# Down projection with a zero-padded last weight chunk kept twice, and int8 staging replaced by int16 in place

## The chip, the cores and the metric

The kernel runs on one core of a Trainium2 chip. The metric is the device time of one execution in microseconds; the profile is one further execution, recorded by the hardware profiler. TensorE (PE) multiplies, VectorE (DVE), ScalarE (ACT) and GpSimd (POOL) work on elements, SyncE (SP) issues DMAs. A line number such as L1046 is a line of the kernel's file as profiled before.

## The reference, cut to what matters

The input x is 64 sequences of 64 tokens with 256 channels. A rotation, a decayed linear attention with its residual and a pooled softmax over tokens come first; then a feed-forward layer, quantized to 8-bit integers, is added to x. This last part is what the change touches:

```python
xq = _act_fake_quant(x, clip_x[0])
gate = jnp.einsum('bsh,ih->bsi', xq, _weight_fake_quant(w_gate))
up = jnp.einsum('bsh,ih->bsi', xq, _weight_fake_quant(w_up))
h = _act_fake_quant(jax.nn.silu(gate) * up, clip_down[0])
return jnp.einsum('bsi,hi->bsh', h, _weight_fake_quant(w_down))
```

`_act_fake_quant` takes one scale over the whole tensor (sigmoid of the clip factor, times the largest magnitude, over 127), divides, rounds, clips to -128 to 127 and multiplies by the scale again. `w_gate` and `w_up` are 704 x 256, `w_down` is 256 x 704. The integers are exact in bf16, so the matmuls run on bf16 integers and the scales are applied afterwards.

## The kernel before

The 4096 tokens are cut into 8 groups (`NG`) of 512 tokens (`GW`), each 4 tiles of 128 tokens. The attention phase works through the groups in a hand-written order, with the preparation of the weights spread over its steps: `weight_round` (ACT, to int8), `weight_widen` (DVE, int8 to bf16) and `weight_transpose` (PE, with ACT copying the result out of PSUM). `w_down` is the third of them and comes last, in the step near 131 us.

The inner width of 704 is cut into 6 chunks (`NC`): five of 128 rows and a last one of 64 (`LAST`). Groups are paired: pair j holds groups 2j and 2j + 1. The inner layer of a pair lies in `hT[j]`, 11 rows (`NF + 1`) of 128 partitions x 512 tokens in f32: rows 0, 2, 4, 6, 8 are the five full chunks of the even group, rows 1, 3, 5, 7, 9 those of the odd group, and row 10 (`NF`) holds the 64-row last chunk of the even group on partitions 0 to 63 and that of the odd group on partitions 64 to 127. The quantized copy `hq[j]` has the same layout in bf16; its pool keeps two such tiles, so pair j + 2 takes the place of pair j. The down weights `wdT` lie in chunks of 128 partitions x 256 outputs; their last chunk holds the 64 rows twice, on both halves of the partitions.

Before the down projection the feed-forward part multiplies gate and up. Its input integers come from `quantize_tokens`: ACT multiplies by the inverse scale and writes int8 (L959), and DVE (groups 0 and 1) or POOL (the others) widens to bf16 (L961). The largest magnitude of the inner layer is collected on DVE; `act_scale` turns it into `sh` and its inverse `rh`. Only then can the down projection begin:

- `quantize(g)`: ACT multiplies `hT` by `rh` and writes int8 into `h8` (L1046); DVE widens that into `hq` (L1047). The even group also does row 10 for both groups, as a separate instruction of its own. The first group is cut into 1, 1 and 2 token tiles, the last into 2 and 2; all others are done at once.
- `down(g)`: for each of 4 token tiles, 6 matmuls (L1060) accumulate over the chunks, the last with only 64 rows of the array. Two tiles share a PSUM tile `pdn` (4 buffers). DVE multiplies each by the output scale `dsc` (L1067) into the residual's tile. For groups 0 to 6 POOL issues an accumulating DMA onto the output (L1076), which the attention phase has already stored; for group 7 DVE adds the residual (L1072) and SP issues two plain stores (L1073).

The order on ACT, DVE and POOL is that of the code (`manual_schedule`): `quantize(g)` is written ahead of `down(g - 1)`, so on DVE the widening of group g stands ahead of the two evictions of group g - 1. PE's order and all waits come from the framework, which follows what each instruction reads and writes.

Of the kernel before, what the change touches and what calls it, by code (L numbers as in the profile page):

```python
# [10 lines left out]
BF16 = mybir.dt.bfloat16  # L11
I32 = mybir.dt.int32
I8 = mybir.dt.int8
AF = mybir.ActivationFunctionType
ALU = mybir.AluOpType
AX = mybir.AxisListType

P = 128
NEG = -1e30
QMAX = 127.0  # L20
# [6 lines left out]
def adaln_attn_ffn(  # L27
# [20 lines left out]
    nc = tc.nc  # L48
    B, S, D = x.shape
# [3 lines left out]
    FF = w_gate.shape[0]  # L53
# [4 lines left out]
    GW = GT * P  # L58
# [3 lines left out]
    NC = (FF + P - 1) // P  # L62
    LAST = FF - (NC - 1) * P
# [4 lines left out]
    const = ctx.enter_context(tc.tile_pool(name="const", bufs=1))  # L68
# [20 lines left out]

    wgT = const.tile([P, 2, FF], BF16, name="wgT")  # L90
    wuT = const.tile([P, 2, FF], BF16, name="wuT")
    wdT = const.tile([P, NC, D], BF16, name="wdT")
    wscale = const.tile([P, 2, NC], F32, name="wscale")
    dsc = const.tile([P, D], F32, name="dsc")

# [14 lines left out]
    with ExitStack() as actx:  # L110
# [22 lines left out]
        pooled = [pool_a[:, g] if g < 5 else pool_b[:, g - 5] for g in range(NG)]  # L133
# [8 lines left out]
        def scale_ys(g):  # L142
            if g == 0:

                ys = pool.tile([P, GT, D], F32, tag="ys", name="ys_0", bufs=1)
                for t in range(GT):
                    nc.scalar.activation(
                        ys[:, t], xg[0][:, t], AF.Copy, scale=cs[:, 1, t : t + 1]
                    )
# [67 lines left out]
        def keys(g):  # L217
# [3 lines left out]
            for r in range(2):  # L221
                pk = by_token(g, r, wkT, "pk")
                sq = pool.tile([P, 512], F32, tag="sq", name=f"sq_{g}_{r}")
                nc.scalar.activation(sq, pk, AF.Square)
                nc.vector.tensor_reduce(
# [312 lines left out]
        with tc.tile_pool(name="prep", bufs=1) as prep:  # L538
# [22 lines left out]
            for k in range(2):  # L561
                rows = slice(k * A, (k + 1) * A)
# [9 lines left out]
            row, tok = p32("row", 1), p32("tok", 1)  # L572
# [3 lines left out]
            for k in range(P // 32):  # L576
                rows = slice(32 * k, 32 * (k + 1))
                V.tensor_scalar_add(row[rows], sq32[rows, 0:1], 32.0 * k)
            V.tensor_scalar(ident, col, row, None, ALU.is_equal)
            for k in range(2):  # L580
                rows = slice(k * S, (k + 1) * S)
# [32 lines left out]
            for k in range(2):  # L614
                rows = slice(k * S, (k + 1) * S)
# [48 lines left out]
            w, pt = turn(wkT, wq_nat, center, 2)  # L664
# [3 lines left out]
            w, pt = turn(wqT, wq_nat, ident, 0)  # L668
# [24 lines left out]
            for k in range(2):  # L693
                rows = slice(k * S, (k + 1) * S)
# [5 lines left out]
            w, pt = turn(wvT, wq_nat, ident, 4)  # L700
# [14 lines left out]
            w, pt = turn(woT, wo_nat, ident, 0)  # L715
# [6 lines left out]
            for k in range(2):  # L722
                half = slice(k * A, (k + 1) * A)
                V.tensor_scalar_mul(vb[half, half], ones[half, half], v1s[half])

        wprep = actx.enter_context(tc.tile_pool(name="wprep", bufs=1))


        full = (NC - 1) * P
        wnat, wint = [], []  # L730
        for j, w in enumerate((w_gate, w_up)):
# [17 lines left out]
        w8 = [  # L749
            wprep.tile(list(nat.shape), I8, tag="w8", name=f"w8_{j}")  # L750
            for j, nat in enumerate(wnat)
# [19 lines left out]
        def weight_widen(j):  # L771
            if j < 2:
                q = wprep.tile([P, NC, D], BF16, tag="wq", name=f"wq_{j}")
                nc.vector.tensor_copy(q, w8[j])
            else:
                q = wprep.tile([P, 2, NC * P], BF16, tag="wq", name="wq_d")
                nc.vector.tensor_copy(q[:, :, 0:FF], w8[j])
                nc.vector.tensor_copy(q[:, :, FF : NC * P], q[:, :, full:FF])

                for hc in range(2):  # L780
                    nc.vector.tensor_scalar_mul(
                        wnat[2][:, hc, 0:P], ident, sd[:, hc : hc + 1]
                    )
                nc.vector.memset(wnat[2][:, 0, P : 2 * P], 1.0)
            wint.append(q)

        def weight_transpose(j):
            q = wint[j]
            if j < 2:
                for kc in range(2):  # L790
                    pt = ps.tile([P, 1024], BF16, tag="bank", name=f"pw_{j}_{kc}")
                    for c in range(NC):
                        n = P if c < NC - 1 else LAST
                        nc.tensor.transpose(
                            pt[:, c * P : c * P + n],
                            q[:n, c, kc * P : (kc + 1) * P],
                            identb[:n, :n],
                        )
                    nc.scalar.copy((wgT, wuT)[j][:, kc, :], pt[:, :FF])
                return  # L800
            pd = bank("pdsc")
            for hc in range(2):
                nc.tensor.matmul(
                    pd[:, hc * P : (hc + 1) * P],
                    wnat[2][:, 0, P : 2 * P],
                    wnat[2][:, hc, 0:P],
                    start=True,
                    stop=True,
                )
            nc.scalar.copy(dsc, pd[:, :D])  # L810
            for hc in range(2):
                pt = ps.tile([P, 1024], BF16, tag="bank", name=f"pwd_{hc}")
                for c in range(NC):
                    nc.tensor.transpose(
                        pt[:, c * P : (c + 1) * P], q[:, hc, c * P : (c + 1) * P], identb
                    )
                nc.scalar.copy(
                    wdT[:, :, hc * P : (hc + 1) * P],
                    pt[:, : NC * P].rearrange("p (c h) -> p c h", h=P),
                )  # L820


        for step in range(1, NG):
            p, a, q = step, step - 1, step - 2
# [52 lines left out]
        a, q = NG - 1, NG - 2  # L877
# [42 lines left out]
        rx = const.tile([P, 1], F32, name="rx")  # L920
# [3 lines left out]
    with ExitStack() as fctx:  # L924
# [5 lines left out]
        NF = 2 * (NC - 1)  # L930
        ps_f = ctx.enter_context(ExitStack())
        fw = ps_f.enter_context(tc.tile_pool(name="ffnw", bufs=2))
# [3 lines left out]
        xq = fp.tile([P, 2, NT], BF16, name="xq")  # L936
        hT = [
            (fp if j < NP - 1 else big).tile(
                [P, NF + 1, GW], F32, tag=f"hT{j}" if j < NP - 1 else "last", name=f"hT{j}"
            )  # L940
            for j in range(NP)
        ]
# [10 lines left out]
        )  # L953
        wsx = fp.tile([P, 2, NC], F32, name="wsx")

        def quantize_tokens(g, kcs=slice(0, 2)):

            x8 = fw.tile([P, 2, GW], I8, tag="x8", name=f"x8_{g}_{kcs.start}", bufs=4)
            nc.scalar.activation(x8[:, kcs], pooled[g][:, kcs], AF.Copy, scale=rx)  # L959
            widen = nc.vector if g < 2 else nc.gpsimd  # L960
            widen.tensor_copy(xq[:, kcs, g * GW : (g + 1) * GW], x8[:, kcs])  # L961

        for kc in range(2):
            for g in range(2):
# [14 lines left out]
        for j in range(NP):  # L979
            for c in range(NC):  # L980
# [4 lines left out]
                for dst, w in ((pg, wgT), (pu, wuT)):  # L985
                    for kc in range(2):
                        for k in range(2):
                            g = 2 * j + k
# [11 lines left out]
                h = hT[j][:, 2 * c : 2 * c + n, :]  # L1000
# [18 lines left out]
        fw = fctx.enter_context(tc.tile_pool(name="ffnd", bufs=2))  # L1019
# [5 lines left out]
        rh = fp.tile([P, 1], F32, name="rh")  # L1025
# [3 lines left out]
        hq = {}  # L1029

        def quantize(g):

            j, k = divmod(g, 2)
            if k == 0:
                hq[j] = fw.tile([P, NF + 1, GW], BF16, tag="hq", name=f"hq_{j}")

            h8 = fw.tile([P, NC, GW + 64], I8, tag="h8", name=f"h8_{g}")
            at = 0
            for n in (1, 1, 2) if g == 0 else (2, 2) if g == NG - 1 else (4,):
                cols = slice(at * P, (at + n) * P)  # L1040
                at += n
                for rows, tmp in (
                    (slice(NF, NF + 1), h8[:, NC - 1 : NC, cols]),
                    (slice(k, NF, 2), h8[:, 0 : NC - 1, cols]),
                )[k:]:
                    nc.scalar.activation(tmp, hT[j][:, rows, cols], AF.Copy, scale=rh)  # L1046
                    nc.vector.tensor_copy(hq[j][:, rows, cols], tmp)  # L1047

        def down(g):
            j, k = divmod(g, 2)  # L1050

            res = xg[0 if g == NG - 1 else g]
            for r in range(2):
                tiles = slice(2 * r, 2 * r + 2)
                pdn = ps_d.tile([P, 2, D], F32, tag="pdn", name=f"pdn_{g}_{r}")
                for i in range(2):
                    tok = slice((2 * r + i) * P, (2 * r + i + 1) * P)
                    for c in range(NC):
                        half = slice(0, P) if c < NC - 1 else slice(k * LAST, (k + 1) * LAST)
                        nc.tensor.matmul(  # L1060
                            pdn[:, i, :],
                            hq[j][half, 2 * c + k if c < NC - 1 else NF, tok],
                            wdT[half, c, :],
                            start=(c == 0),
                            stop=(c == NC - 1),
                        )
                nc.vector.tensor_tensor(  # L1067
                    res[:, tiles], pdn, dsc.unsqueeze(1).to_broadcast([P, 2, D]), ALU.mult
                )
                if g == NG - 1:  # L1070
                    xr = xg[g][:, tiles, :]
                    nc.vector.tensor_tensor(xr, xr, res[:, tiles], ALU.add)  # L1072
                    nc.sync.dma_start(out=ot[g][:, tiles, :], in_=xr)  # L1073
            if g < NG - 1:

                nc.gpsimd.dma_start(out=ot[g], in_=res, accum_op=ALU.add)  # L1076
# [53 lines left out]
```

## Time and profile before

| | us |
|---|---|
| median of 3 runs | 336.67 (335.77 to 337.44) |
| profiled execution, its own time | 336.96 |
| its span in the profile | 335.2 |
| down projection: from the first ACT instruction of `quantize` to the last DVE add | 296.83 to 330.50 |
| last output data landed | 334.0 |

Busy time over the whole span: PE 286.9 us (86%), DVE 244.2 (73%), ACT 197.6 (59%), POOL 84.9 (25%). The span is what lies between the first and the last instruction on the core; the execution's own time is 1.8 us longer. The shares are means over stages that differ: the down projection is the last tenth of the span, so it has to be read by itself. Matmuls overlap, so their mean duration is longer than their distance; the distance is read from their starts.

### The profile page before, as it was taken

The numbers are of one execution on the slowest core, as the hardware profiler recorded it, in microseconds if no ns is written. First come the engines' busy times: TensorE is split into PE (matmuls) and PEld (weight loads), VectorE is DVE, ScalarE is ACT, GpSimd is POOL, SyncE is SP. The second block draws the span as 40 slices with busy tenths as digits, with TensorE's granted clock in tenths as the row PEclk, the third lists the DMA queues.
The fourth block names the chain that finished last, engine by engine and source line by source line (L and its number), as shares of the span: only waits on it lengthen the run. The fifth ranks groups of instructions, "written<-read, shape, count | busy, mean of one in ns | idle before, by whom it ended". The sixth has DMA issues, their size and how long they took to land.

```text
span 335.2 us, 8697 instructions
## 1 busy us (share of the span) xinstructions
PE 286.9 (86%) x3760; PEld 194.9 (58%) x3764; DVE 244.2 (73%) x510; ACT 197.6 (59%) x303; POOL 84.9 (25%) x76
## 2 busy tenths in 40 slices
PE   0599999999999999989999999975498898549992
PEld 0386768668658758848858858653333243115551
DVE  5669886886976985794894694765528789968883
ACT  1566458567476573774574574323668988559820
POOL 0051330240230221014003003040037746503541
PEclk9999999999999999999999999998589999958997
DMA  5590711001001000100100200200000000001999
GB/s 156 128 350 19 218 60 62 5 2 65 3 2 61 8 0 5 62 3 3 65 2 2 66 2 0 68 1 3 0 2 0 1 0 2 0 0 17 164 154 166
DMA packets 16789, 16.15 MB, mean 48 GB/s; under 512 B 2160, under 2 KB 16496, under 8 KB 16752
## 3 DMA queue, kind: packets, MB, share of 16 engines
q1 hardware_dynamic: 12480, 11.83, 11.4%
q0 software_dynamic: 3696, 3.67, 8.2%
q8 instruction: 29, 0.48, 0.6%
q10 hardware_dynamic: 576, 0.11, 0.2%
q14 instruction: 8, 0.07, 0.1%
HBM read 7.74 MB, written 7.86 MB: 47 GB/s over the span
## 4 chain that ended last, share of the span: by engine, by line
PE 53%; DVE 21%; ACT 15%; issue 5%; DMA 3%; POOL 2%; ACTq 0%; DVEq 0%
PE po L388 9%; PE pv L208 9%; PE pdn L1060 7%; PE pk L208 6%; PE psc L323 4%; PE py L361 4%; DVE at L336 4%; ACT gate L997 3%; ACT L238 3%; PE pl L511 3%; DMA afb<-n_L_cond_amplitudes_dram 3%; PE pa L433 2%; POOL hT L1006 2%; ACT up L1003 2%; DVE xam L528 2%
## 5 line engine op out<-in xcount | busy, mean ns | idle before, releaser
L336 DVE TENSOR_TENSOR at<-psc,gam 128x512 f32<-128x512 f32 x64 | 39.6, 680 | 14.6 <-PE psc L323 14.6
L154 POOL TENSOR_TENSOR ys<-x,cs 128x1024 f32<-128x1024 f32 x7 | 13.8, 1967 | 89.3 <-DVE xr L168 67.6
L388 PE MATMUL po<-woT,yT 128*128 128x256 f32 x128 | 31.1, 386 | 5.2 <-DVE kn L254 2.7
L1006 POOL TENSOR_TENSOR hT<-gate,up 128x1024 f32<-128x1024 f32 x10 | 23.7, 2370 | 37.3 <-ACT up L1003 37.3
L1060 PE MATMUL pdn<-wdT,hq 128*128 128x256 bf16 x192 | 30.1, 291 | 3.0 <-DVE hq L1047 3.0
L208 PE MATMUL pk<-wkT,xT 128*128 128x256 f32 x128 | 30.2, 390 | 0.2 <-ACT xT L198 0.2
L989 PE MATMUL pg<-xq,wgT 128*128 128x512 bf16 (+1 forms) x94 | 25.9, 399 | 4.7 <-DVE xq L961 2.2
L208 PE MATMUL pv<-wvT,xT 128*128 128x256 f32 x128 | 29.8, 386 | 0.1
L388 PEld LDWEIGHTS po<-woT,yT 128*128 128x128 f32 x128 | 23.1, 190 | 11.2 <-DVE kn L254 5.1
L283 PE MATMUL pq<-xT,wqT 128*128 128x512 f32 x64 | 29.5, 604 | 0.0
L997 ACT ACTIVATE gate<-pg,wsx 128x1024 f32<-128x1024 f32 (+1 forms) x24 | 24.7, 1054 | 6.8 <-PE pg L989 5.0
L1046 ACT ACTIVATE h<-hT,rh 128x2560 int8<-128x2560 f32 (+5 forms) x17 | 22.3, 1387 | 8.5 <-DVE rh L107 7.3
L410 POOL TENSOR_TENSOR bias<-pre,sel 128x256 f32<-128x256 f32 x8 | 4.9, 612 | 86.7 <-DVE ms L459 86.7
L208 PEld LDWEIGHTS pk<-wkT,xT 128*128 128x128 f32 x128 | 24.3, 196 | 3.9 <-ACT xT L198 0.9
L1060 PEld LDWEIGHTS <-hq 128*128 128x128 bf16 x192 | 16.7, 101 | 16.5 <-issue 10.9
L208 PEld LDWEIGHTS pv<-wvT,xT 128*128 128x128 f32 x128 | 23.7, 190 | 4.5 <-issue 1.4
L972 DVE TENSOR_REDUCE ham<-hT 128x1 f32<-128x1024 f32 (+1 forms) x24 | 26.1, 1121 | 0.2 <-POOL hT L1006 0.2
L989 PE MATMUL pu<-xq,wuT 128*128 128x512 bf16 (+1 forms) x94 | 23.6, 385 | 1.7 <-DVE hT L1008 1.7
L1008 DVE SCALAR_TENSOR_TENSOR hT<-pu,wsx,gate 128x1024 f32<-128x1024 f32 (+1 forms) x14 | 15.8, 1129 | 11.0 <-ACT gate L997 10.8
L291 ACT ACTIVATE qbd<-pq,hm 128x512 f32<-128x512 f32 x32 | 20.1, 679 | 4.9 <-PE pq L283 4.8
L323 PE MATMUL psc<-qbd,kT 32*64 32x128 f32 x1024 | 20.7, 279 | 0.6 <-DVE at L336 0.3
L377 ACT ACTIVATE yT<-py,hm 128x256 f32<-128x256 f32 x32 | 13.4, 470 | 11.5 <-PE py L361 11.5
(180 smaller groups left out, 537.8 us busy)
## 6 DMA issues: line engine op xcount, KB each, us to landing
x<-in_x_dram SPq DMA_DIRECT2D x8, 512.0 KB, 6.4
out_dram<-x SPq DMA_DIRECT2D x7, 512.0 KB, 4.5
out_dram<-x POOLq DMA_DIRECT2D x7, 512.0 KB, 6.6
wq_nat<-in_L_attn_W_qkv_dram SPq DMA_DIRECT2D x3, 256.0 KB, 8.6
wnat_d<-in_L_ffn_w_down_dram SPq DMA_DIRECT2D x1, 704.0 KB, 6.3
wnat<-in_L_ffn_w_gate_dram SPq DMA_DIRECT2D x1, 640.0 KB, 4.6
wnat<-in_L_ffn_w_up_dram SPq DMA_DIRECT2D x1, 640.0 KB, 6.0
out_dram<-x SPq DMA_DIRECT2D x2, 256.0 KB, 4.3
```

Source lines behind the costliest of these rows:

```text
L208: nc.tensor.matmul(pk[:, i * D : (i + 1) * D], xT[:, kc, t * P : (t + 1) * P], w[:, kc, :], start=(kc == 0), stop=(kc == 1),)
L283: nc.tensor.matmul(pq, wqT[:, kc, hf * P : (hf + 1) * P], xT[:, kc, :], start=(kc == 0), stop=(kc == 1),)
L291: nc.scalar.activation(qbd[:, hf, :, k, :], pq.rearrange("p (b s) -> p b s", s=S), AF.Copy, scale=hm[:, k : k + 1],)
L323: nc.tensor.matmul(banks[p][k * S : (k + 1) * S, i, hf, :], kT[rows, hf, b * S : (b + 1) * S], qbd[rows, hf, b].rearrange("p k t -> p (k t)"),
L336: nc.vector.tensor_tensor(at[:, p].rearrange("p i f k t -> p i (f k t)"), banks[p].rearrange("p i f c -> p i (f c)"), gam[:, p] .rearrange ...
L388: nc.tensor.matmul(po[:, i * D : (i + 1) * D], yT[:, i, hf].rearrange("p k t -> p (k t)"), woT[:, hf, :], start=(hf == 0), stop=(hf == 1),)
L972: nc.vector.tensor_reduce(ham[:, nham : nham + 1], h, AX.XY, ALU.max, apply_absolute_value=True)
L989: nc.tensor.matmul(dst[:, k, :] if wide else dst[k * LAST : (k + 1) * LAST, 0, :], w[:, kc, c * P : min((c + 1) * P, FF)], xq[:, kc, g * G ...
L997: nc.scalar.activation(gate[:, :n], pg[:, :n], AF.Silu, scale=wsx[:, 0, c : c + 1])
L1006: nc.gpsimd.tensor_tensor(h, gate, up, ALU.mult)
L1046: nc.scalar.activation(tmp, hT[j][:, rows, cols], AF.Copy, scale=rh)
L1060: nc.tensor.matmul(pdn[:, i, :], hq[j][half, 2 * c + k if c < NC - 1 else NF, tok], wdT[half, c, :], start=(c == 0), stop=(c == NC - 1),)
```

## The change

The last chunk of the down weights is kept in two versions, each filled up to 128 rows with zeros: one with the 64 weights on partitions 0 to 63 and zeros below, one with zeros above and the weights on 64 to 127. `wdT` grows from 6 to 7 chunks. All matmuls of `down` then contract 128 rows: the even group uses chunk 5 and the odd group chunk 6, both against row 10 of `hq[j]`, and the zeros cancel the other group's half. The preparation gains a memset of the zeros and one transpose more for each half of the outputs.

A new helper `integers` takes the place of int8 staging in `quantize` and for token groups 0 and 1: ACT writes int16 into the destination's own bytes (the bf16 tile seen as int16), and DVE clips to -128 to 127 in place and writes bf16. In `quantize` the even group does its six rows, row 10 among them, in one instruction. Tokens of groups 2 to 7 keep int8 and POOL, with two buffers `x8` instead of four.

```diff
-    wdT = const.tile([P, NC, D], BF16, name="wdT")
+    wdT = const.tile([P, NC + 1, D], BF16, name="wdT")
...
-                q = wprep.tile([P, 2, NC * P], BF16, tag="wq", name="wq_d")
+                q = wprep.tile([P, 2, (NC + 1) * P], BF16, tag="wq", name="wq_d")
                 nc.vector.tensor_copy(q[:, :, 0:FF], w8[j])
-                nc.vector.tensor_copy(q[:, :, FF : NC * P], q[:, :, full:FF])
+                nc.vector.memset(q[:, :, FF : FF + P], 0.0)
+                nc.vector.tensor_copy(q[:, :, FF + P :], q[:, :, full:FF])
...
-                for c in range(NC):
+                for c in range(NC + 1):
                     nc.tensor.transpose(
                         pt[:, c * P : (c + 1) * P], q[:, hc, c * P : (c + 1) * P], identb
                     )
                 nc.scalar.copy(
                     wdT[:, :, hc * P : (hc + 1) * P],
-                    pt[:, : NC * P].rearrange("p (c h) -> p c h", h=P),
+                    pt[:, : (NC + 1) * P].rearrange("p (c h) -> p c h", h=P),
                 )
...
+        def integers(dst, src, inv):
+            d16 = dst.bitcast(I16)
+            nc.scalar.activation(d16, src, AF.Copy, scale=inv)
+            nc.vector.tensor_scalar(dst, d16, QMAX, -QMAX - 1.0, ALU.min, ALU.max)
+
         def quantize_tokens(g, kcs=slice(0, 2)):
-            x8 = fw.tile([P, 2, GW], I8, tag="x8", name=f"x8_{g}_{kcs.start}", bufs=4)
+            dst = xq[:, kcs, g * GW : (g + 1) * GW]
+            if g < 2:
+                integers(dst, pooled[g][:, kcs], rx)
+                return
+            x8 = fw.tile([P, 2, GW], I8, tag="x8", name=f"x8_{g}")
             nc.scalar.activation(x8[:, kcs], pooled[g][:, kcs], AF.Copy, scale=rx)
-            widen = nc.vector if g < 2 else nc.gpsimd
-            widen.tensor_copy(xq[:, kcs, g * GW : (g + 1) * GW], x8[:, kcs])
+            nc.gpsimd.tensor_copy(dst, x8[:, kcs])
...
-            h8 = fw.tile([P, NC, GW + 64], I8, tag="h8", name=f"h8_{g}")
+            rows = slice(k, NF + 1 - k, 2)
             at = 0
             for n in (1, 1, 2) if g == 0 else (2, 2) if g == NG - 1 else (4,):
                 cols = slice(at * P, (at + n) * P)
                 at += n
-                for rows, tmp in (
-                    (slice(NF, NF + 1), h8[:, NC - 1 : NC, cols]),
-                    (slice(k, NF, 2), h8[:, 0 : NC - 1, cols]),
-                )[k:]:
-                    nc.scalar.activation(tmp, hT[j][:, rows, cols], AF.Copy, scale=rh)
-                    nc.vector.tensor_copy(hq[j][:, rows, cols], tmp)
+                integers(hq[j][:, rows, cols], hT[j][:, rows, cols], rh)
...
-                        half = slice(0, P) if c < NC - 1 else slice(k * LAST, (k + 1) * LAST)
+                        last = c == NC - 1
                         nc.tensor.matmul(
                             pdn[:, i, :],
-                            hq[j][half, 2 * c + k if c < NC - 1 else NF, tok],
-                            wdT[half, c, :],
+                            hq[j][:, NF if last else 2 * c + k, tok],
+                            wdT[:, c + k if last else c, :],
```

More of the change, by code (lines that the diff above doesn't have):

```diff
@@ L13 @@
 I8 = mybir.dt.int8
+I16 = mybir.dt.int16
 AF = mybir.ActivationFunctionType
```

## The prediction

> **What bounds the kernel now.** I read the chain of waits from 286 us on first, then the timeline, the groups by shape and the DMA view of that stretch, because the change's main edits lie in the down projection, the last stage. The chain (start, length, what) carries it:
>
> ```profile
> 296.83 6.11 ACT h L1046 x7
> ...
> 302.96 1.77 DVE hq L1047
> ...
> 304.78 24.29 PE pdn L1060 x168
> ...
> 329.09 0.70 DVE x L1067
> ...
> 329.81 0.69 DVE x L1072
> ```
>
> Rounding and casting of the first two groups fill 8 us. Then TensorE runs 168 matmuls (seven groups of 24) without a wait: 24.29 / 7 = 3.46 us a group, 0.1446 us a matmul. Its weight loads in the timeline:
>
> ```profile
> 305.43 0.65 PEld L1060 LDWEIGHTS <-hq 64*128 64x128 bf16 x6 [0.21 <-issue]
> 306.29 0.65 PEld L1060 LDWEIGHTS <-hq 64*128 64x128 bf16 x6 [0.21 <-issue]
> ```
>
> Each line is a run of six loads beginning with the 64-row one; runs repeat every 0.865 us and each is preceded by a 0.21 us hole. In the single records of the trace the full-height matmuls start 0.109 us apart (305.76, 305.87, 305.98), while the start of the 64-row one and of the one after it each come 0.20 to 0.21 us after their predecessor. So the mixed heights cost 0.865 - 6 x 0.109 = 0.21 us per output tile.
>
> The other engines, by shape (count | busy us, mean ns):
>
> ```profile
> L1046 ACT ACTIVATE h<-hT,rh 128x2560 int8<-128x2560 f32 x6 | 14.3, 2413 | 0.0
> ...
> L1067 DVE TENSOR_TENSOR x<-pdn,dsc 128x512 f32<-128x512 f32 x16 | 10.7, 682 | 3.0 <-PE pdn L1060 3.0
> L1047 DVE CAST hq<-h 128x2560 bf16<-128x2560 int8 x6 | 10.5, 1750 | 1.1 <-ACT h L1046 1.1
> ...
> L1047 DVE CAST hq<-h 128x512 bf16<-128x512 int8 x3 | 1.2, 416 | 0.0
> ```
>
> Neither limits today: per two groups ACT needs 5.34 us (starts 303.45, 305.76, 308.08, 308.70 in the records) and DVE 0.42 + 2 x 1.75 + 4 x 0.60 (evictions start to start) = 6.3 us, against TensorE's 6.91. TensorE's clock (second to last figures: clock, DMA share, GB/s) is halved until 304.07:
>
> ```profile
> 300.00:304.00 4.00, 4.00 (x17) 1.97 (x17) 2.25 (x3) 4.00 (x4) 0.00 (x0) 0.50 0.00 0
> 304.00:308.00 4.00, 3.75 (x26) 2.00 (x24) 4.00 (x6) 4.00 (x2) 1.77 (x1) 0.99 0.00 0
> ```
>
> The fourth resource does not stand in the chain. The DMA view of 300 to 336 us, in 40 slices of 0.9 us:
>
> ```profile
> DMA  0000000003999999999999995999999997999600
> GB/s 0 0 0 0 0 0 0 0 0 20 110 159 200 155 167 197 165 92 137 188 185 146 197 197 56 80 187 199 160 160 200 173 98 68 196 201 359 226 0 0
> ...
> out_dram<-x POOLq DMA_DIRECT2D x7, 512.0 KB, 6.6
> out_dram<-x SPq DMA_DIRECT2D x2, 256.0 KB, 4.3
> ```
>
> Once the first accumulating store starts, its 16 engines are never free: plateaus of 195 to 200 GB/s with a slow stretch at the head of each store. By the packet records the seven stores begin at 308.74, 312.25, 315.40, 318.90, 322.21, 325.71 and 328.68, each where the one before ends; the last group's two plain stores get their packets only from 332.30 (issued at 328.80 and 330.53) and land at 334.0. So DMA is a second, nearly equal bound: 3.32 us a store.
>
> [...]
>
> **The change part by part.**
>
> *All rows contracted.* Same 24 matmuls a group, all 128 rows high: 24 x 0.109 = 2.61 us, 0.84 less. In the half-clock group 0 the pitch is 0.213, 5.11 us plus the waits for data.
>
> *Quantizing.* ACT: [...] 5 rows 2.41 and 2.31: 5.05 per two groups. I take int16 output to cost what int8 does; [...] DVE clip: [...] I take 950. DVE per two groups: 1.9 + 4 x 0.60 = 4.3. TensorE needs 5.2: still the slowest compute engine, by 0.2 over ACT.
>
> *The wait that is added.* ACT now writes hq itself; hq has two buffers of two groups, so ACT for group 4 waits for the matmuls of group 1, group 6 for those of 3; behind it on ACT's queue stand only later groups. By the steps below group 1's matmuls end at 306.6 while ACT reaches group 4 at 307.3, and those of 3 at 311.8 against 312.3: nothing is held. At clips of 1.75 us ACT would be held some 0.5 us and DVE would end at 325.6, still ahead of the DMA below.
>
> *The steps.* Group 0: ACT 296.83 to 297.75, 298.57, 300.03; clips done 298.13, 298.95, 300.61; matmuls from 298.2 (298.68 before) to 303.4. Group 1: ACT until 302.34, clip until 303.32 (the cast ended at 304.72), matmuls 303.4 to 306.4, clock full from 304.07. From there 2.61 a group: the last matmul at about 322.1, last DVE add at 323.8 instead of 330.50. **Compute alone would save 6.7 us.**
>
> *DMA takes part of it back.* Group 0's second eviction ends at 304.55 (305.91). POOL's issue:
>
> ```profile
> 306.23 1.94 POOL L1076 DMA_DIRECT2D out_dram<-x  x1 [15.92 <-DVE x L1067]
> 309.41 1.61 POOL L1076 DMA_DIRECT2D out_dram<-x  x1 [1.24 <-DVE x L1067]
> ```
>
> 0.32 after the eviction, 1.3 to 1.9 long (I take 1.5), first packet 0.57 after its end: 306.95, 1.8 earlier. Stores are then asked for every 2.61 us, but 512 KB at the plateau of 195 GB/s is 2.63 plus the slow head. Heads differ: stores that found the queue free (first, third, fifth) took 3.5 us, those already waiting behind another (second, fourth, sixth) 2.96 to 3.15. With all later ones waiting I take 3.05: 3.5 + 6 x 3.05 = 21.8, plus 1.65 for the last 512 KB of plain stores as before: end at 306.95 + 23.4 = 330.4 against 334.0. **Saving 3.6.** With no heads at all it ends at 327.9 (saving 6.1); with heads as now (6 x 3.32 + 3.94, + 1.4) at 332.2 (saving 1.8).
>
> *Elsewhere.* Tokens of groups 0 and 1: [...] only the last lies ahead of a matmul: at most 0.15 saved, taken as 0.1. Token rounding for g>=2 has two buffers instead of four; the first cast on POOL ended at 251.84 and its buffer is rewritten at 260.94: nothing, with 9 us of cover. Weights, once near 131 us: a memset of 256 elements on DVE (the one of 128 took 165 ns; about 0.3), hidden in DVE's idle time before 135.99; two more transposes at 0.055, of which one batch waits for ACT's dsc copy anyway: +0.06; two copies on ACT 0.1 longer each, ahead of xT copies that have 1.4 us of slack. Sum +0.05, with 0 to 0.4 as bounds (0.4 if none of it is covered).
>
> **Sum.** -3.6 - 0.1 + 0.05 = -3.6 us. The profiled execution took 336.96 us (span 335.2, 1.8 around it), so 333.3 for it; the median of the runs, 336.67, is 0.3 lower: **333.1**. About 0.5%, 1.7 us, is what a measurement here can tell from no change.
>
> **Rivals.**
> 1. *DMA keeps pace* (0.20): waiting stores lose their heads and compute sets the end: 6 to 6.9 saved, 330. For: the plateau's 2.63 equals the 2.61 asked for. Against: even waiting stores had heads of 0.3 to 0.5.
> 2. *DMA gives nothing back* (0.10): heads as now, only the earlier start counts: 1.8 saved, 334.9.
> 3. *The holes stay* (0.04): they come from something other than height. Then only the earlier start remains, 1.0 saved, 335.7. Against: they sit on the 64-row matmuls alone.
> 4. *DVE becomes the bound, slower* (0.06): [...] It decides once clips take over 4.5 us per two groups, 0.80 ns an element [...]. [...]
> 5. *ACT waits for TensorE inside one hq tile, slower* (0.03): the rows of groups 2j and 2j+1 interleave; were they taken to overlap, ACT and TensorE would alternate, some 5 us worse, 342. Against: the cast of group 1 began at 302.96 while group 0's matmuls read the same tile until 304.5.
>
> **Numbers.** The likeliest case has 0.57, from 331 to 335 us by the two ends of the DMA estimate. Leaving out part of the fastest and all slower cases, 329.4 to 335.6 holds 8 in 10. Faster by over 0.5%: likeliest 0.57, rival 1 0.20, rival 2 and a little of 3 0.08, so 0.85; within: the rest of both, 0.06; slower: rivals 4 and 5, 0.09.
>
> **What would show it.** Right: load runs with no 0.21 hole, matmul pitch 0.109; clips near 950 ns; the last DVE add near 324; a gap between it and the end of the span that grows from 4.7 to about 8 us, filled with DMA at 160 to 175 GB/s. Wrong: clips of 2.8 us or more; ACT idle before group 4; the gap staying 4.7 (rival 1); a pitch still 0.145 (rival 3).

## The result, and the profile after

The changed kernel takes 332.55 us (median of 4 runs, 331.60 to 333.34) where the kernel before took 337.06 in the same comparison: ratio 0.9879, 95% interval 0.9841 to 0.9918. A second set of runs of the same kernel gave 332.20 against 335.85, ratio 0.9874 (0.9850 to 0.9899). The ratio is an estimate from the single runs and not the quotient of the two medians; those quotients, 0.9866 and 0.9891, lie inside the intervals. Carried to the median before of 336.67, the two ratios are 4.1 and 4.2 us saved (the medians themselves differ by 4.5 and 3.7); 3.6 had been forecast.

The profiled execution took 331.6 us with a span of 329.9, 5.3 below the span before. To compare executions I count from the end of the instruction that makes the inverse scale `rh` ("from `rh`", 296.71 us before and 295.74 after), since the down projection can only begin there. Line numbers in the views are from here on those of each kernel's own file. The chain of waits of the changed kernel, with start, length and what:

```profile
295.86 0.94 ACT hq L964
...
296.82 0.37 DVE hq L965
...
297.33 13.30 PE pdn L1069 x96
...
310.64 9.36 PE pdn L1069 x84
...
322.08 0.69 DVE x L1081
```

The first clip takes 0.37 us and TensorE begins 1.59 us from `rh` (1.97 before). The last VectorE add ends at 322.77, 27.03 from `rh`; before it was 33.79. TensorE's weight loads in the timeline of that stretch:

```profile
302.45 7.88 PEld L1069 LDWEIGHTS <-hq 128*128 128x128 bf16 x72 [0.32 <-DVE hq L965]
310.64 10.38 PEld L1069 LDWEIGHTS <-hq 128*128 128x128 bf16 x96 [0.31 <-DVE hq L965]
```

There are no more runs of six with a hole ahead of each: 96 loads in 10.38 us, 0.108 each. What ends the two idle gaps left is a clip on VectorE. The groups by shape (count | busy us, mean ns | idle before):

```profile
L1085 POOL DMA_DIRECT2D out_dram<-x x7 | 10.5, 1506 | 21.1 <-DVE x L1076 21.1
L964 ACT ACTIVATE hq<-hT,rh 128x3072 int16<-128x3072 f32 x3 | 8.5, 2840 | 0.0
L964 ACT ACTIVATE hq<-hT,rh 128x2560 int16<-128x2560 f32 x3 | 7.2, 2412 | 0.0
...
L965 DVE TENSOR_SCALAR hq<-hq 128x3072 bf16<-128x3072 int16 x3 | 3.3, 1085 | 1.3 <-ACT hq L964 1.3
L965 DVE TENSOR_SCALAR hq<-hq 128x2560 bf16<-128x2560 int16 x3 | 2.9, 953 | 1.7 <-ACT hq L964 1.7
```

The clip of five rows takes 953 ns where the cast took 1750. Five and six rows cost the same; the mean of 1085 for six is two clips of 960 and one of 1336. 3072 elements in 960 ns are 0.31 ns an element, where the cast's 2560 in 1750 were 0.68. ACT never waits for TensorE in these rows. The DMA view from 295 us on, in slices of 0.9 us:

```profile
DMA  0000000000003999999999999999999999995000
GB/s 0 0 0 0 0 0 0 0 0 0 0 0 33 97 177 200 183 188 197 187 157 200 196 197 200 186 195 200 195 178 193 199 215 240 233 245 184 5 0 0
...
out_dram<-x POOLq DMA_DIRECT2D x7, 512.0 KB, 7.4
out_dram<-x SPq DMA_DIRECT2D x2, 256.0 KB, 6.0
```

The queue is full from the first store to the end, without the dips to 56 and 68 GB/s that the view before showed, and a store now lands 7.4 us after its issue (6.6 before). The last data land at 328.50, 5.73 us after the last add; before, 3.51 after it. By the packet records the accumulating stores begin at 306.50, 309.87, 312.65, 315.52, 318.17, 320.90 and 323.65.

### The profile page after: what moved, and what is told of

Same layout as the page of the kernel before. It is cut to its first block, busy times and chain, and to the rows that moved or that the text cites. A ratio compares the mean times of both kernels' runs of the same rounds, so it can differ in the third digit from the quotient of the medians.

```text
span 329.9 us, 8696 instructions
## 1 busy us (share of the span) xinstructions
PE 280.2 (85%) x3766; PEld 197.4 (60%) x3766; DVE 236.3 (72%) x505; ACT 196.6 (60%) x297; POOL 83.7 (25%) x76
## 4 chain that ended last, share of the span: by engine, by line
PE 53%; DVE 21%; ACT 13%; issue 5%; DMA 3%; POOL 2%; ACTq 1%; DVEq 0%
PE po L389 9%; PE pv L209 9%; PE pdn L1069 7%; PE pk L209 5%; PE psc L324 4%; PE py L362 4%; DVE at L337 4%; ACT gate L1011 3%; ACT L239 3%; PE pl L512 3%; DMA lgb<-in_L_attn_log_gamma_dram 3%; PE pa L434 2%; ACT up L1017 2%; POOL hT L1020 2%; DVE xam L529 2%
## 5 line engine op out<-in xcount | busy, mean ns | idle before, releaser
L209 PE MATMUL pk<-wkT,xT 128*128 128x256 f32 x128 | 29.5, 383 | 0.2 <-ACT xT L199 0.2
L1069 PE MATMUL pdn<-wdT,hq 128*128 128x256 bf16 x192 | 23.9, 292 | 2.4 <-DVE hq L965 2.4
L1003 PE MATMUL pu<-xq,wuT 128*128 128x512 bf16 (+1 forms) x96 | 24.4, 387 | 1.7 <-DVE hT L1022 1.7
L964 ACT ACTIVATE hq<-hT,rh 128x2560 int16<-128x2560 f32 (+4 forms) x11 | 20.9, 1987 | 7.3 <-DVE rh L108 7.3
L1069 PEld LDWEIGHTS <-hq 128*128 128x128 bf16 x192 | 19.7, 104 | 6.7 <-issue 2.6
```

The source lines that it names most:

```text
L209: nc.tensor.matmul(pk[:, i * D : (i + 1) * D], xT[:, kc, t * P : (t + 1) * P], w[:, kc, :], start=(kc == 0), stop=(kc == 1),)
L964: nc.scalar.activation(d16, src, AF.Copy, scale=inv)
L1003: nc.tensor.matmul(dst[:, k, :] if wide else dst[k * LAST : (k + 1) * LAST, 0, :], w[:, kc, c * P : min((c + 1) * P, FF)], xq[:, kc, g * G ...
L1069: nc.tensor.matmul(pdn[:, i, :], hq[j][:, NF if last else 2 * c + k, tok], wdT[:, c + k if last else c, :], start=(c == 0), stop=(c == NC ...
```

## The experiments

Lengths below are from one profiled execution of each kernel. "Stage" is from `rh` to the last VectorE add, "tail" from there to the end of the span, and their sum is what the down projection costs with its stores. Ratios are to the kernel before, run beside each (its medians 335.85 to 337.06; the median of the row "before" is that of the three runs of the table further up).

| kernel | median us | ratio (95%) | stage | tail | sum |
|---|---|---|---|---|---|
| before | 336.67 | | 33.79 | 4.74 | 38.53 |
| changed | 332.55 | 0.9879 (0.9841 to 0.9918) | 27.03 | 7.12 | 34.15 |
| changed, second set | 332.20 | 0.9874 (0.9850 to 0.9899) | 27.03 | 7.82 | 34.85 |
| padding only | 334.95 | 0.9939 (0.9917 to 0.9960) | 30.23 | 6.30 | 36.53 |
| int16 only | 335.89 | 0.9975 (0.9954 to 0.9996) | 33.05 | 4.54 | 37.59 |
| changed, no accumulating stores | 328.68 | 0.9743 (0.9709 to 0.9777) | 26.88 | 3.00 | 29.88 |
| before, no accumulating stores | 335.27 | 0.9950 (0.9926 to 0.9974) | 33.79 | 3.00 | 36.79 |
| int16, 64-row matmuls side by side | 332.87 | 0.9893 (0.9868 to 0.9918) | 30.09 | 5.03 | 35.12 |
| residual added on POOL | 334.58 | 0.9939 (0.9915 to 0.9962) | 32.42 | 3.44 | 35.86 |
| POOL adds groups 1, 3, 5 | 332.83 | 0.9887 (0.9862 to 0.9913) | 29.32 | 5.79 | 35.11 |
| tokens only | 336.36 | 1.0000 (0.9983 to 1.0016) | 33.79 | 4.63 | 38.42 |
| plain stores, no add | 329.20 | 0.9774 (0.9738 to 0.9809) | 26.96 | 3.07 | 30.03 |
| VectorE adds group 6 | 331.03 | 0.9841 (0.9812 to 0.9871) | 27.27 | 6.13 | 33.40 |
| VectorE adds groups 3, 6 | 330.31 | 0.9826 (0.9797 to 0.9856) | 28.16 | 4.69 | 32.85 |

**Each half alone.** Padding only: the kernel before with the seven weight chunks and 128-row matmuls, int8 staging and casts kept.

```diff
...
-                            hq[j][half, 2 * c + k if c < NC - 1 else NF, tok],
-                            wdT[half, c, :],
+                            hq[j][:, NF if last else 2 * c + k, tok],
+                            wdT[:, c + k if last else c, :],
...
```

> The zero-padded chunk alone, int8 staging kept everywhere. Theory A (the 64-row matmuls' holes set the pace): the matmul pitch falls to 0.109 us, but DVE then needs 6.3 us per two groups (casts 0.42 + 2 x 1.75, four evictions of 0.60) against TensorE's 5.2, so groups come every 3.15 us instead of 3.46: 2 us saved, ratio 0.994, and TensorE waits for the casts. Theory B (the cheaper DVE work makes the gain): nothing to speak of, under 0.5 us.

The holes go, but the stage falls by 3.56 us only. The timeline of the weight loads and the waits (engine, line, what it waited for: us in total, times, longest) say what took their place:

```profile
308.10 2.52 PEld L1071 LDWEIGHTS <-hq 128*128 128x128 bf16 x24 [0.68 <-DVE hq L1058]
310.96 2.52 PEld L1071 LDWEIGHTS <-hq 128*128 128x128 bf16 x24 [0.34 <-DVE hq L1058]
```

```profile
PE pdn L1071 <- DVE hq L1058: 4.7, 6, 2.7
```

A group of 24 loads takes 2.52 us without a hole and then TensorE waits 0.34 to 0.68 for VectorE's cast. A pair of groups comes every 6.05 us (308.10 to 314.15; 6.3 had been expected): VectorE, with casts of 1.75 us, works without a pause in this stretch and has become the slowest engine.

Int16 only: the changed kernel with the 64-row last chunk of before.

```diff
...
-                            hq[j][:, NF if last else 2 * c + k, tok],
-                            wdT[:, c + k if last else c, :],
+                            hq[j][half, 2 * c + k if c < NC - 1 else NF, tok],
+                            wdT[half, c, :],
...
```

> int16 in place alone (inner layer and token groups 0 and 1), last chunk still 64 rows high. Theory A: holes of 0.21 us stay, a group still takes 3.46 us on TensorE, only the start of the stage is earlier by 1 us or so: ratio 0.996 to 0.997. Theory B: most of the 4.5 us of the whole change, ratio 0.988 to 0.990.

```profile
304.23 0.65 PEld L1068 LDWEIGHTS <-hq 64*128 64x128 bf16 x6 [0.21 <-issue]
```

```profile
ACT hq L963 <- PE pdn L1068: 1.7, 1, 1.7
```

The 0.21 us holes are all there in the timeline, and a group takes 3.46 us as before. The stage gains 0.74, all of it at its start: the first clip is shorter and TensorE begins 1.59 us from `rh` instead of 1.97, and by the single records the second group follows the first after 5.73 us instead of 6.09. The waits show the one place where quantizing in place costs something: TensorE being slower, ACT once waits 1.7 us for it to release `hq`. TensorE itself was not late by it: it waits for VectorE only once, at its start.

So the halves save 3.56 and 0.74 us of the stage, 4.30 together, and 6.76 when both are made: each removes the limit that the other would run into.

**What the stores cost.** The accumulating stores are taken out of both kernels.

```diff
-            if g < NG - 1:
-                nc.gpsimd.dma_start(out=ot[g], in_=res, accum_op=ALU.add)
```

> The changed kernel without the accumulating stores of groups 0 to 6 (their feed-forward part does not reach the output). Theory A (DMA takes back 2.4 us of what the matmuls save): last DVE add at the same place, 26.9 us after the stage's first ACT instruction, and the time from it to the end of the span falls from 7.1 to about 4 us: 3 us less than the changed kernel, ratio 0.979. Rival (the long end is a fixed cost or the plain stores' own latency): the end stays near 7 us and the ratio near 0.988.

> The kernel before without the accumulating stores of groups 0 to 6 (their feed-forward part does not reach the output). Theory A: TensorE's pitch is unchanged and the end falls from 4.7 to about 4 us: 0.7 us less, ratio 0.998. Rival (DMA was the real bound before, too): the end loses as much as in the changed kernel, 3 us, ratio 0.991.

The DMA view of the changed kernel without them, in the same slices:

```profile
DMA  0000000000000000000000000000000358000000
GB/s 0 0 0 0 0 0 0 0 0 0 0 0 0 0 18 0 0 0 0 0 0 0 0 0 0 0 0 0 0 0 0 118 173 286 6 0 0 0 0 0
```

Only the last group's two plain stores are left, and the tail is 3.00 us in both kernels. The sum falls by 1.74 us before (38.53 to 36.79) and by 4.27 after (34.15 to 29.88). In the kernel before only 0.7 had been expected: the stores lengthened its end, too, though less than in the changed kernel. Computing alone, then, became 6.91 us shorter, and the stores take 2.5 of it back (3.2 by the second profile of the changed kernel).

**Bytes or addition.** The stores of groups 0 to 6 become plain stores of the same size from SP; they overwrite the output instead of adding to it.

```diff
-                nc.gpsimd.dma_start(out=ot[g], in_=res, accum_op=ALU.add)
+                nc.sync.dma_start(out=ot[g], in_=res)
```

> The changed kernel with the seven accumulating DMAs replaced by plain stores of the same bytes from SP (the attention residual of groups 0 to 6 is overwritten, not added to). If it is the accumulation that fills the DMA engines, a plain store of 512 KB takes about 1.4 us instead of 2.76 (both rates from the runs so far), no store waits, and the end is 3.0 us as without stores: ratio 0.975. If it is the bytes as such, the end stays above 5 us.

```profile
DMA  0000000000001941963934925916906944800000
GB/s 0 0 0 0 0 0 0 0 0 0 0 0 65 352 166 61 328 192 133 348 121 144 349 89 177 349 56 209 347 26 238 339 162 135 291 0 0 0 0 0
...
out_dram<-x SPq DMA_DIRECT2D x7, 512.0 KB, 2.9
```

The bytes are the same, but slices reach 349 GB/s, the engines idle between the stores, and a store lands 2.9 us after its issue. The sum is 30.03, within 0.15 us of no stores at all. So it is not the number of bytes that fills the queue but the way they are stored: by the packet records, 1 KB takes 102 ns at the median in the accumulating stores and 48 in the plain ones. The run changes two things at once, though, the addition and the engine that issues (POOL before, SP now, with another DMA queue). No run here has a plain store issued by POOL, so how much each of the two costs is not shown; below, "accumulating store" means both together.

**Holes by switch or by height.** The int16 kernel keeps its 64-row matmuls, but in every second token tile the 64-row one goes first, so that two of them follow each other.

```diff
...
+                    chunks = range(NC) if i == 0 else [NC - 1, *range(NC - 1)]
-                    for c in range(NC):
+                    for c in chunks:
...
```

> int16 in place, last chunk 64 rows high as in the kernel before, but every second token tile begins with that chunk, so that two 64-row matmuls stand side by side and the height changes half as often. If the change of height costs [...], holes of 0.21 us come once per two tiles: a group takes 3.03 us instead of 3.46, the stage to the last DVE add 29.7 us instead of 33.05, the DMA end grows to some 6.5, ratio 0.991. If each 64-row matmul costs by itself, nothing moves against int16 alone: ratio 0.9975.

```profile
305.87 0.11 PEld L1069 LDWEIGHTS <-hq 64*128 64x128 bf16 x2 [0.21 <-issue]
306.19 0.99 PEld L1069 LDWEIGHTS <-hq 128*128 128x128 bf16 x10 [0.21 <-issue]
307.39 0.11 PEld L1069 LDWEIGHTS <-hq 64*128 64x128 bf16 x2 [0.21 <-issue]
```

Two tiles now take 1.52 us (305.87 to 307.39) instead of 2 x 0.865 = 1.73, which is 12 x 0.109 and one 0.21. The cost belongs to the excursion from 128 rows and back, not to the 64-row matmul: two that stand together pay it once. The trace shows this cost of 0.21 us, not what TensorE does in it. The stage is 30.09 us (29.7 expected) and the tail 5.03 (6.5 expected). With no padded weights the kernel is at 0.9893, whose interval overlaps that of the change, since the tail falls as the stage grows.

**The residual elsewhere.** If the accumulating stores hold the end, another engine may add. First POOL, for groups 0 to 6, with SP storing the sum; the attention phase's own store of these groups then falls away.

```diff
...
-                nc.gpsimd.dma_start(out=ot[g], in_=res, accum_op=ALU.add)
+                nc.gpsimd.tensor_tensor(xg[g], xg[g], res, ALU.add)
+                nc.sync.dma_start(out=ot[g], in_=xg[g])
...
```

> The changed kernel without accumulating DMAs: DVE evicts to a tile of its own, POOL adds the residual for groups 0 to 6 and SP stores plainly; the stores in the attention phase are gone. If the accumulating stores alone stretch the end, it falls from 7.1 to 3.0 us: 4 us less than the changed kernel, ratio 0.975, provided POOL's add (about 2 us, estimated from its multiplies of the same size) and DVE's clips do not hold one another up. If they do, a group takes about 2.95 us instead of 2.61 and 2 us are lost again: ratio 0.981.

A miss: 0.9939, worse than the change itself. The groups by shape and the timeline:

```profile
L1082 POOL TENSOR_TENSOR x<-x,res 128x1024 f32<-128x1024 f32 x7 | 18.8, 2700 | 18.2 <-DVE res L1074 18.2
...
L963 DVE TENSOR_SCALAR hq<-hq 128x3072 bf16<-128x3072 int16 x3 | 5.7, 1914 | 0.6 <-ACT hq L962 0.6
```

```profile
303.60 2.35 POOL L1082 TENSOR_TENSOR x<-x,res 128x1024 f32<-128x1024 f32 x1 [14.41 <-DVE res L1074]
304.02 2.74 DVE L963 TENSOR_SCALAR hq<-hq 128x3072 bf16<-128x3072 int16 x1 [0.60 <-ACT hq L962]
```

The clip begins 0.4 us after POOL's add and ends at 306.76, 0.81 us after the add has ended (305.95); alone it takes 0.96. Its mean rises from 1085 to 1914 ns, POOL's add from 2.35 us (the first) to 2.70 at the mean, and TensorE waits for VectorE again. So the two engines slow each other here; by what means is not shown. At the end of the stage the two clips of the last group, 0.55 us each in the changed kernel, take 2.04 at the mean, and one of VectorE's own two adds takes 2.33 instead of 0.69 beside an add on POOL. I then let POOL add in groups 1, 3 and 5 only.

```diff
+ADD = (1, 3, 5)
...
+            if g in ADD:
+                nc.gpsimd.tensor_tensor(xg[g], xg[g], res, ALU.add)
+                nc.sync.dma_start(out=ot[g], in_=xg[g])
+            elif g < NG - 1:
```

> The changed kernel with the accumulating DMA kept for groups 0, 2, 4 and 6 and POOL's add with a plain store for 1, 3 and 5. The DMA engines get 4 x 2.76 + 3 x 1.4 us of work instead of 7 x 2.76, so no store should wait for another: end 3.0 to 3.7 us after the last DVE add, stage 27.0 to 27.9; 3 to 4 us less than the changed kernel, ratio 0.976 to 0.979. If the end is a matter of the last store alone and not of the backlog, it stays near 7.

```profile
313.07 2.34 POOL L1087 TENSOR_TENSOR x<-x,res 128x1024 f32<-128x1024 f32 x1 [0.51 <-DVE res L1079]
313.12 3.12 DVE L966 TENSOR_SCALAR hq<-hq 128x2560 bf16<-128x2560 int16 x1
```

A miss as well: 0.9887, no better than the change. The stage grows by 2.3 us to 29.32, the tail falls by 1.3 to 5.79 where 3.0 to 3.7 had been expected, and in the profile the sum is 35.11. Lengthened clips, like the one above (3.12 us instead of 0.95), take what the shorter queue gives.

Then VectorE adds, as it does for group 7 already, in group 6 alone, and in groups 3 and 6.

```diff
+ADD = (3, 6)
...
-                if g == NG - 1:
+                if g == NG - 1 or g in ADD:
                     xr = xg[g][:, tiles, :]
                     nc.vector.tensor_tensor(xr, xr, res[:, tiles], ALU.add)
                     nc.sync.dma_start(out=ot[g][:, tiles, :], in_=xr)
-            if g < NG - 1:
+            if g < NG - 1 and g not in ADD:
```

> The changed kernel with group 6 treated as group 7 is: DVE adds the residual (two adds of 0.69 us) and SP stores plainly, no accumulating DMA. DMA work falls by 2.76 - 1.4 = 1.4 us, DVE's last add comes up to 0.7 us later; if the backlog of the stores sets the end, about 1.3 us less than the changed kernel, ratio 0.984; if it does not, 0 to 0.7 us more.

> The same for groups 3 and 6. Stores no longer queue up: DMA alone would end 2.7 us earlier than in the changed kernel; DVE's adds of 1.4 us at group 3 are absorbed by its 0.45 us of idle time a group over the next three. 2 to 2.7 us less than the changed kernel, ratio 0.980; if DVE cannot absorb them, 1 us less at most.

```profile
DMA  0000000000029999999999959799999999300000
GB/s 0 0 0 0 0 0 0 0 0 0 0 25 88 149 197 168 166 193 190 196 197 212 352 205 66 119 193 190 175 196 199 330 384 384 106 0 0 0 0 0
```

With groups 3 and 6 on VectorE, 0.9826, the queue slackens once in the middle, and of its last megabyte, stored plainly, slices go out at up to 384 GB/s. The stage costs 1.13 us more, the tail is 2.43 less. Group 6 alone: 0.24 more and 0.99 less, 0.9841.

```profile
PEld L1072 <- DVE hq L966: 2.1, 5, 1.0
```

So most of the 1.13 comes from group 3. Its adds stand on VectorE ahead of the clip that group 5 needs, and TensorE waits 1.0 us for that clip, the longest of its five waits there. The sum falls by 1.3 us instead of the 2 to 2.7 expected.

**The change once more**, to stand beside these with as many runs.

> The changed kernel once more, unaltered, so that it has as many runs as the versions it is set against. Two ways of dividing the output (groups 3 and 6 added on VectorE, ratio 0.9826; group 6 alone, 0.9841) stood ahead of its 0.9879, but the intervals overlapped. Theory (the accumulating stores hold the end): 0.988 with an interval of some 0.003, above 0.9856, the upper end of the version with groups 3 and 6; in the profile a stage of 27.0 us from the inverse scale to the last VectorE add and 7 us of stores behind it. Rival (the versions differ by nothing that can be measured): 0.984 or below.

The ratio is 0.9874, and the stage 27.03 us to the hundredth, with output stores that fill 22.6 us of DMA (22.0 in the first profile). Adding groups 3 and 6 on VectorE lies 0.0048 below; the two half widths of 0.0025 and 0.003 combine to 0.004, so it is ahead by some 1.6 us at the edge of what these runs can tell, and it has the lowest ratio of the versions that compute the whole output; group 6 alone (0.9841) cannot be told from it.

**Tokens alone.** The kernel before with the int16 route for token groups 0 and 1 only.

```diff
...
+            if g < 2:
+                d16 = dst.bitcast(I16)
+                nc.scalar.activation(d16, pooled[g][:, kcs], AF.Copy, scale=rx)
+                nc.vector.tensor_scalar(dst, d16, QMAX, -QMAX - 1.0, ALU.min, ALU.max)
+                return
...
```

> The kernel before with int16 in place for token groups 0 and 1 only. By the clip alone the first gate activation comes 0.13 us earlier after the scale (5.95 to 5.82 us); in the changed kernel it came 0.47 earlier. If the rest is where TensorE's clock happens to be restored, this run lies anywhere from 5.3 to 5.8 with the restoration; if the clip does it all, 5.48. The stage after is as before. Ratio 0.999.

```profile
L963 DVE TENSOR_SCALAR xq<-xq 128x512 bf16<-128x512 int16 x4 | 1.2, 294 | 1.8 <-ACT xq L962 1.8
```

A clip of 512 elements takes 294 ns (the cast 426), and the first matmul comes 1.31 us after the tokens' inverse scale `rx` instead of 1.44. The time is the same to 0.17%.

## Why the prediction was right, step by step

The likeliest case came about, and its steps can be set against the traces one by one.

- **Holes.** Predicted: 0.21 us per output tile gone, 24 matmuls in 2.61 us. Measured: starts 0.109 us apart, the last four groups begin 2.62 to 2.63 us apart on TensorE. Padding only and the side-by-side version show that the change of height was the cause; rival 3 falls.
- **Quantizing.** ACT's five rows 2.41 us predicted, 2412 ns measured; two groups 5.05 predicted, 5.06 to 5.07 between starts measured. The six rows within that took 2840 ns; a line through the 640 and 2560 elements of the kernel before (812 and 2413 ns) gives the same 2.84 us. VectorE's clips 950 predicted, 943 to 960 measured for five and six rows, but for one of 1336. The 950 was my estimate: the trace before has no instruction on int16. Rival 4 (a slow clip) falls; the 2.8 us it was to be known by was an estimate too. A slip without effect: ACT's 5.34 us per two groups before is 5.25 by the starts that stand beside it.
- **The added wait.** ACT was predicted never to be held by the two `hq` buffers, and in the changed kernel it isn't. That this hangs on TensorE's pace was shown by int16 only, where it waits 1.7 us; rival 5 falls.
- **Computing alone saves 6.7 us.** 6.76 by the stage, 6.91 by the two kernels without accumulating stores. Group 0's second eviction, put 7.84 us from `rh`, came at 7.85; the last add, put at 27.09, came at 27.03. TensorE sets the pace from the second group on, as predicted: from there groups begin 2.75, 2.63, 2.81, 2.63, 2.62 and 2.62 us apart, where the 2.75 holds the last matmuls at half clock (0.5 granted until 302.73, 1.0 from then on) and the 2.81 a short wait for the clip of 1336 ns. In the second profile the stage was 27.03 as well; there the second group waited for its clip (done at 303.96, first matmul at 304.00, 6.70 from `rh`; 6.71 in the first profile).
- **The first store.** Put 1.8 us earlier; from `rh` it started 1.27 earlier (12.03 to 10.76). The eviction was right; the mis-sized term is POOL's issue, for which I took 1.5 us out of 1.3 to 1.9, and which took 2.02, nearly as in the kernel before (1.94).
- **The stores.** The other mis-sized term. Waiting stores were put at 3.05 us; the five that can be read between starts took 2.78, 2.87, 2.65, 2.73 and 2.75, and 2.75 on average in the second profile. At the plateau of 195 GB/s a store would take 2.63, so the slow head almost vanished here where the next store already waited: rival 1's argument, which I had weighed too low. Why waiting stores had a longer head in the kernel before is not shown. With the first store at 3.37 (3.5 predicted) and the last with the plain ones at 4.85 (4.7), DMA takes 22.0 us instead of 23.4, and 22.6 in the second profile. The two mis-sized terms have opposite signs, 0.5 us too early a start and 0.8 to 1.4 too long a drain, and in part cancel: that the forecast of 3.6 lies so near the measured time owes something to luck.
- **What DMA gives back.** Put at 3.1 us (6.7 less 3.6). The stretch from the last add to the last landing grew by 2.2 (3.51 to 5.73), and by 2.8 in the second profile (6.35). Rival 1 (computing sets the end) had nothing here and rival 2 (heads as before) 4.9; neither holds. The gap to the end of the span, 7.12 and 7.82, was put at about 8; its DMA rate, put at 160 to 175 GB/s, was 184 to 245 in the first profile.
- **Tokens and weights.** Put at -0.1, my estimate as well, and +0.05. The tokens' clip brings 0.13. The first profile shows 0.47 less between `rx` and the first gate (5.95 to 5.48), but the second only 0.13; the rest goes with the moment when TensorE's clock is restored, 5.75 us after `rx` before and 4.91 in that execution. With tokens only, which has the same clip, the clock came back at 5.42, the first gate at 5.73, and the time is no different, so this part is not the change's. From the start of the `w_down` cast to that of the instruction that makes `rx` it is 0.06 to 0.08 us longer with the padded weights (109.26 before, 109.32 to 109.34 in three profiles).

The sum against the first profile: stage -6.76, tail +2.38, tokens -0.47, weights +0.08, and -0.6 that arises ahead of the weights' step, where nothing was edited: -5.4, against 5.3 less span. What the ratios of the runs give, 4.1 and 4.2 us, lies between the two changes of the sum, -4.38 and -3.68.

## What to carry to other kernels

Before a speed-up of the last stage is booked, count what its output queue needs: here computing gained 6.8 us, and a queue of accumulating stores that needs 2.7 us for each 2.6 us of work gave 2 to 3 of them back. Two edits that relieve different engines of one loop can be worth more together than the sum of each alone (6.8 against 4.3), so try them as a pair. When the queue is the bound, spread its work over engines with idle time, but look at which of them slow each other: beside POOL's add a clip took 2.74 us instead of 0.96.

## What the runs showed of the hardware that was not expected

- Accumulating stores of 512 KB, issued by POOL, drained at one per 2.65 to 2.9 us when queued, about 190 GB/s; plain ones of the same size, issued by SP, reached 349 GB/s in a slice and left the queue idle.
- VectorE's int16 clip (0.95 us alone) took 2.74 and 3.12 us where it began during a two-input add on POOL (2.35 us for 128x1024). One of VectorE's own two-input adds, 0.69 otherwise, took 2.33.
- Two 64-row matmuls side by side among 128-row ones cost 0.21 us once, together.
- One of the six-row clips took 1336 ns in both profiles of the changed kernel. In the first it ran (309.25 to 310.58) while POOL issued a store (309.02 to 310.81), in the second likewise (310.80 to 312.14, within 310.57 to 312.36). The same clip took 1336 ns, again 0.23 us after the start of such an issue, in both versions that add on VectorE, and 960 and 964 ns in the two that issue nothing on POOL. So the longer time goes with an issue on POOL, but not with every one: another clip that ran within an issue took 959. Why is open.
